# Reordering one stage of a graph-layer kernel: the guess behind the sort, GpSimd's gathers and second secant at the last chunk, a new prologue

## Chip, cores, metric

One core of a Trainium2 chip. The metric is device time in microseconds (us), the median of several executions. Runs of one batch share a chip and the runs of the kernel before that are timed on it. The times differ from chip to chip: the kernel before takes 3235 and 3237 us on two of those used and 3456 us on a third (whether that was the chip or a passing state of it was not tested), so numbers of two batches are compared as ratios or by the loop's own tile length, which is the same (40.95 us in a profile that spans 3454.9 us, 40.93 in one of 3226.0).

## The reference, cut to what matters

Four graph layers on 4096 rows of 256 features, each with a residual and a layernorm. The change lies in the second of two steps of layer 1:

```python
for n in range(2):
    A  = top_p_attention(Xa)   # softmax of q k^T; keep the largest entries of
                               # each row until 90% of its mass; renormalise
    Xf = R @ Xf                # R: sparse adjacency + identity, rows normalised
    Xa = A @ Xa
    Z  = Z + Xf @ U1[n].T + Xa @ U2[n].T
out = layernorm(X + Z)         # then the layer's own residual and layernorm
```

The cut at 90% of the mass is what costs. The kernel finds it per row without sorting 4096 entries: it guesses a bound h from two sums, refines it twice by a secant (each needs two sums over the tile of exponentials), takes 48 candidates below the bound in order, and finds the cut among them.

## The kernel before

Step two works tile by tile (128 rows, 32 tiles) and spreads four tiles over one pass of the loop. While TensorE forms the weighted sum of tile I in eight chunks, the logits of tile I+3 are made, the bound of tile I+2 is refined twice, tile I+1 is sorted and cut, and tile I-1 goes through its projection pz and two layernorms (`end`, in six steps). In this loop the engines run in the order in which the code is written, as the trace has it: VectorE's L754, L881 and L758 start at 2472.09, 2477.39 and 2478.16, and GpSimd's rows below stand in it too.

```python
steps(first); steps(few); run(first)   # tile I+2: secant 1; tile I+1: half the candidates
# slots, one per chunk g of the weighted sum of tile I (TensorE):
#   g 0-3: logits chunk of tile I+3      every g: one matmul of R's sum
#   g 4  : sums for the refinement (L619); end 1     g 5: end 6 of tile I-2
#   g 6  : second of these sums (L621);    end 2 (pz on TensorE)
steps(few)                             # other half of the candidates
if new: guess(new)                     # needs the sums of ALL four logits chunks
new_xa(...); run(r)
if new: run(new["sums"])               # ScalarE: two sums for the guessed bound
run(few)                               # the sort part (VectorE, 8 us)
steps(end)                             # end 3: statistics of pz (VectorE), rs (GpSimd)
ahead = r_ahead(b + 1, got); steps(ahead)   # GpSimd: five gathers for the next R
steps(second)                          # GpSimd: secant 2 of tile I+2, 13 small instructions
c = cut(tile I+1); steps(c)            # VectorE: L754, eight times (e > tie) * e
steps(end)                             # end 4: y = (pz - m) * rs (VectorE L881), GpSimd: * g + x
run(c)                                 # VectorE: match-replace on the whole tile (L758)
steps(end); run(second)                # end 5: statistics of y; new bound h
```

TensorE's next tile begins with the transposes of the tile that was just cut.

## Time and profile before

| | kernel before |
|---|---|
| time | 3234.09 us (3 runs, 3232.30 to 3242.01) |
| step two, one steady tile | 40.95 us |
| VectorE's waits in it | 5.6 us |
| TensorE's wait in it | 10.3 us |

The prediction shows the page's slices, the chain of one tile and VectorE's waits. In all views PE is TensorE, DVE is VectorE, ACT is ScalarE, POOL is GpSimd, and L12 is line 12 of the kernel; rs is one over the standard deviation of a layernorm, st its statistics. One more view belongs beside them: GpSimd's timeline of the same tile (columns are start, length, engine, line, operation, output and inputs; in brackets the idle time before and what ended it).

```profile
2467.68 0.19 POOL L715 COPY f_x<-ex 128x1 f32<-128x1 f32 x1 [4.90 <-DVE ex L714]
...
2470.20 0.57 POOL L240 TENSOR_TENSOR rs<-ve,neg_half 128x1 f32<-128x1 f32 x1
2470.94 1.14 POOL L355 DMA_INDIRECT xg<-xd,idx_x  x1 [0.17 <-issue]
...
2482.63 0.73 POOL L882 TENSOR_TENSOR y<-y,gb 128x256 f32<-128x256 f32 x1
```

The order to see is: a small copy (L715), then rs of the first layernorm (L240), then the gathers (L355), and only behind the second secant the product for y (L882). Here rs stands ahead of everything slow.

### The profile page before, as it was taken

Reading aid. Unit: us, or ns where it says so; the run is one execution under the profiler, and the core shown is the slowest. Engines: PE = TensorE matmul, PEld = TensorE weight load, DVE = VectorE, ACT = ScalarE, POOL = GpSimd, SP = SyncE. Lnnn points to the kernel's source line nnn. Section 1 sums busy time; section 2 is a strip of 40 time slices with the busy share of each in tenths; the row PEclk is TensorE's granted clock in tenths of the full one; section 3 lists DMA queues with packets and bytes.
Section 4 is the critical chain, followed back from the end, with each engine's and each line's share of the span. In section 5 each row is a group of like instructions: output and inputs, shape, how many; then the busy total and the mean of one; then the engine's idle time right before and its main releaser. Section 6 shows DMA issues by size and latency. Waiting matters only on the chain.

```text
span 3454.9 us, 41436 instructions
## 1 busy us (share of the span) xinstructions
PE 2716.3 (79%) x12372; PEld 2045.6 (59%) x12372; DVE 2318.5 (67%) x7296; ACT 1468.8 (43%) x2399; POOL 1539.0 (45%) x2323
## 2 busy tenths in 40 slices
PE   6776778979999999984777777777777766766777
PEld 5554555756767777762565555555555555554665
DVE  5773559956666666615888888888888884554444
ACT  0000013423333433346777776777777751442110
POOL 1025340046555433343655555555555553554553
PEclk9997888989999999996888888888888878788888
DMA  9964440023322222231211111111111103554443
GB/s 293 295 184 142 131 126 30 12 84 105 106 90 92 85 76 66 64 121 44 66 46 54 47 39 36 38 43 38 38 39 34 37 26 116 177 175 147 142 153 102
DMA packets 346506, 322.83 MB, mean 93 GB/s; under 512 B 32032, under 2 KB 305840, under 8 KB 346272
## 3 DMA queue, kind: packets, MB, share of 16 engines
q1 hardware_dynamic: 281696, 187.30, 18.1%
q0 software_dynamic: 43328, 118.63, 11.4%
q10 hardware_dynamic: 21248, 14.16, 1.3%
q8 instruction: 101, 1.65, 0.2%
q14 instruction: 133, 1.09, 0.1%
HBM read 272.48 MB, written 47.48 MB: 93 GB/s over the span
## 4 chain that ended last, share of the span: by engine, by line
PE 22%; DVE 20%; issue 5%; ACT 2%; POOL 2%; another core or an unknown queue 2%; DMA 1%; POOLq 0%; ACTq 0%; DVEq 0%
PE acc L206 6%; DVE e L754 5%; PE lg L515 4%; DVE e L758 4%; PE pt L195 3%; PE acc L925 2%; PE acc L410 2%; DVE top L708 2%; DVE rest L710 2%; PE pz L830 2%; POOL xg L355 1%; PE acc L1124 1%; PE acc L182 1%; ACT e L583 1%
## 5 line engine op out<-in xcount | busy, mean ns | idle before, releaser
L195 PE MATMUL pt<-ident,e 128*128 128x128 f32 x2048 | 328.6, 293 | 347.3 <-DVE e L758 335.1
L355 POOL DMA_INDIRECT xg<-xd,idx_x x360 | 442.3, 1229 | 260.0 <-PE acc L410 107.6
L197 ACT COPY eT<-pt 128x512 f32<-128x512 f32 x512 | 297.0, 588 | 590.0 <-PE pt L195 529.4
L195 PEld LDWEIGHTS pt<-ident,e 128*128 128x128 f32 x2048 | 271.6, 152 | 401.8 <-issue 359.2
L206 PE MATMUL acc<-x,eT 128*128 128x256 f32 x2048 | 499.2, 388 | 0.3 <-ACT eT L197 0.3
L206 PE MATMUL acc<-xa,eT 128*128 128x256 f32 x2048 | 496.0, 389 | 0.0
L206 PEld LDWEIGHTS acc<-x,eT 128*128 128x128 f32 x2048 | 390.3, 194 | 82.2 <-issue 20.7
L206 PEld LDWEIGHTS acc<-xa,eT 128*128 128x128 f32 x2048 | 403.6, 198 | 59.7
L515 PE MATMUL lg<-kT,qi 64*128 64x512 f32 x1024 | 335.0, 718 | 33.5 <-ACT junk L586 23.2
L583 ACT ACTIVATE e<-lg 128x1024 f32<-128x1024 f32 x256 | 262.3, 1025 | 174.4 <-PE lg L515 158.7
L182 PE MATMUL acc<-xw,panel 128*128 128x257 f32 x1024 | 269.4, 414 | 57.7 <-DMA panel<-in_pair 38.8
L410 PE MATMUL acc<-xg,pc 128*128 128x256 f32 x796 | 259.8, 431 | 29.5 <-DMA xg<-x3d,idx_x 11.3
L182 PEld LDWEIGHTS acc<-xw,panel 128*128 128x128 f32 x1024 | 200.7, 205 | 110.7 <-DMA panel<-in_pair 41.0
L687 DVE MAX8 cand<-e 128x8 f32<-128x128 f32 x1024 | 214.9, 279 | 54.2 <-ACT e L583 49.3
L715 POOL COPY f_x<-ex 128x1 f32<-128x1 f32 x64 | 11.8, 184 | 517.9 <-DVE ex L714 517.9
L619 ACT ACTIVATE junk<-e,hm 128x4096 bf16<-128x4096 f32 x64 | 237.2, 3706 | 10.9 <-DVE hm L614 10.2
L621 ACT ACTIVATE junk<-e,h 128x4096 bf16<-128x4096 f32 x64 | 237.7, 3713 | 1.0
L410 PEld LDWEIGHTS acc<-xg,pc 128*128 128x128 f32 x796 | 144.5, 208 | 118.9 <-issue 70.7
L355 POOL DMA_INDIRECT pc<-in_pair,idx_a x180 | 171.6, 953 | 87.0 <-issue 47.5
L696 DVE MAX8 cand<-tmp 128x8 f32<-128x128 f32 x1024 | 204.3, 277 | 2.2
L355 POOL DMA_INDIRECT xg<-x3d,idx_x x146 | 139.1, 953 | 138.9 <-PE acc L410 61.2
L218 ACT COPY xT<-ptx 128x256 f32<-128x256 f32 (+1 forms) x160 | 73.1, 457 | 291.2 <-DMA panel<-in_pair 120.8
(248 smaller groups left out, 4815.1 us busy)
## 6 DMA issues: line engine op xcount, KB each, us to landing
panel<-in_pair SPq DMA_DIRECT2D x200, 256.0 KB
half<-in_pair SPq DMA_DIRECT2D x64, 512.0 KB
pc<-pk SPq DMA_DIRECT2D x55, 320.0 KB
z<-z SPq DMA_DIRECT2D x128, 128.0 KB
pc<-pk SPq DMA_DIRECT2D x45, 256.0 KB
xin<-xd SPq DMA_DIRECT2D x64, 128.0 KB
xg<-xd,idx_x POOLq DMA_INDIRECT x360
pc<-pk SPq DMA_DIRECT2D x23, 192.0 KB
```

Source lines behind the costliest of these rows:

```text
L182: nc.tensor.matmul(ps[:, :width], a[:, k, :], r, start=(j == 0), stop=(j == NT - 1))
L195: nc.tensor.transpose(pt[:, k, :], e[:, (g * 4 + k) * P:][:, :P], ident)
L197: nc.scalar.copy(eT[g], pt)
L206: nc.tensor.matmul(ps[:, :D], eT[g][:, k, :], rhs[j][:, :D], start=(j == 0), stop=(j == NT - 1))
L355: nc.gpsimd.indirect_dma_start(out=o, out_offset=None, in_=src, in_offset=bass.IndirectOffsetOnAxis(ap=idx[:, c], axis=0))
L410: nc.tensor.matmul(ps[:, :width], pc[:, k, :], xs[k][:, :width], start=(n == 0), stop=stop and n == CAPS[I] - 1)
L515: nc.tensor.matmul(ps[:, h, :], qi[r, :], kT[r, (n * NC + c) * LC:][:, :LC], start=True, stop=True)
L583: nc.scalar.activation(both(e, c), ps, AF.Exp, accum_out=s8[:, c:c + 1])
L619: nc.scalar.activation(junk_tile(), e, AF.Relu, bias=hm, accum_out=part)
L621: nc.scalar.activation(junk_tile(), e, AF.Sign, bias=h, scale=-1.0, accum_out=below)
L687: nc.vector.max(cand[:, g, :], e[:, g * SEG:(g + 1) * SEG])
L696: nc.vector.max(cand[:, c * (NS // 2) + g, :], w[:, g * SEG:(g + 1) * SEG])
```

## The change

Its intent: VectorE should not wait 3.7 us per tile for the guess's inputs while it could sort; GpSimd should use its idle time in the middle of the tile; and the prologue should let the first tiles start earlier.

```diff
# loop of step two
+            ahead = r_ahead(b + 1, got) if 0 <= b + 1 < NT else none    # moved up
             if I + 2 < NT: ...
# in the slots
                     steps(r, n_r)
+                    if g == NT // 4 - 1:          # the last chunk
+                        run(r)
+                        steps(ahead)              # gathers
+                        steps(second)             # second secant
# behind the slots
             steps(few)
-            if new:
-                guess(new)
             if I < NT: new_xa(...)
-            run(r)
-            if new:
-                run(new["sums"])
             run(few)                              # sort part
+            if new:
+                guess(new)
+                run(new["sums"])
             steps(end)
-            ahead = ...; steps(ahead)
-            steps(second)
             c = cut(...)
# prologue: for tiles 0, 1, 2 in a loop  ->  tile by tile
-    for I in range(3): start I, guess I, first secant of I-1, ...
-    run(keep_few(at[0])); run(cut(at[0])); run(secant(at[1], 1))
+    start 0, guess 0; start 1, first secant of 0, guess 1, second secant of 0; keep_few 0;
+    start 2, first secant of 1; cut 0; guess 2; second secant of 1
```

## The prediction

> **What bounds the kernel now.** The page first. The change touches only step two, slices 19 to 33, where VectorE reads 8 tenths and TensorE 7, and the prologue just ahead of it.

> ```profile
> PE   6776778979999999984777777777777766766777
> ...
> DVE  5773559956666666615888888888888884554444
> ...
> L195 PE MATMUL pt<-ident,e 128*128 128x128 f32 x2048 | 328.6, 293 | 347.3 <-DVE e L758 335.1
> ```

> The reader sees that no engine is full, and that TensorE's transposes lose 335 us to VectorE's match-replace (L758). So step two is a loop that goes through several engines, and busy shares will not decide it.

> Next the chain that ended last, for one steady tile (times are us of the profiled span; columns are start, length, what).

> ```profile
> 2478.16 4.50 DVE e L758 x2
> ...
> 2482.80 1.94 PE pt L195 x8
> ...
> 2499.45 1.12 ACT e L583 x2
> 2500.57 1.01 ACT junk L586 x2
> ...
> 2501.60 0.17 DVE q L598
> ```

> The loop closes as: match-replace ends the cut of tile I+1, TensorE transposes it, four logits chunks follow among the weighted sum, ScalarE takes the exponentials of the last, VectorE makes the guess from their sums, then sorts and cuts, and the next match-replace ends 40.95 us later (its rows of L754 start at 2472.09 and 2513.05). Third, the waits of VectorE over the steady loop (total us, times, longest).

> ```profile
> DVE f_s L595 <- ACT e L583: 77.4, 27, 3.5
> DVE st L224 <- POOL y L883: 38.9, 27, 2.0
> DVE q L598 <- ACT junk L586: 22.9, 27, 0.8
> ...
> DVE st L224 <- PE pz L876: 0.8, 3, 0.3
> ```

> The first and third rows are what the change aims at: (77.4 + 22.9) / 27 = 3.7 us per tile, as the guess stands ahead of the sort on VectorE and holds it up. The second, 1.4 us, is the wait for GpSimd's layernorm product. The last row is my main warning: VectorE already waits now and then for the projection pz of the previous tile, so that result comes only just in time.

> To see how just, I took TensorE's, ScalarE's and GpSimd's timelines of the same tile (one row each; columns are start, length, engine, line). I count all times below from the end of match-replace at 2482.66.

> ```profile
> 2509.39 0.59 PE L876 MATMUL pz<-z,ident 128*128 128x256 f32 x2
> ```
> ```profile
> 2508.40 3.71 ACT L621 ACTIVATE junk<-e,h 128x4096 bf16<-128x4096 f32 x1
> ```
> ```profile
> 2477.71 0.19 POOL L629 TENSOR_SCALAR below<-below 128x1 f32<-128x1 f32 x1
> ```

> pz is complete at 2509.98 = 27.3. The second refinement's sums (L621, with a 0.19 us accumulator read) end at 2512.20 = 29.5. The second secant on GpSimd is 13 small instructions, from 2477.71 to 2482.67: 4.96 us with nothing in the way. VectorE reaches the eight cutting instructions (L754) at 2513.05 = 30.4 and leaves them 5.39 later, at 35.8.

> [...] within the hand-scheduled loop all four engines run exactly in the order in which the program emits. [...] in the first tile's cut:

> ```profile
> 1612.51 5.38 DVE L754 SCALAR_TENSOR_TENSOR e<-e,ties 128x512 f32<-128x512 f32 x8
> ```
> ```profile
> 1615.95 2.00 POOL L629 TENSOR_SCALAR below<-below 128x1 f32<-128x1 f32 x1 [6.59 <-ACT junk L621]
> ```

> That GpSimd instruction normally takes 0.19 us (the 2477.71 row). Here it started under L754 and ended at 1617.95, just as the eighth ended (1617.89). At 1657.34 in the next cut, one slipped in at a border between two of the eight (0.49 us) and its successor was held again (1.32 against 0.34). Match-replace has one input, and the secant runs at its usual pace beside it.

> **The change, part by part.**

> 1. Guess behind the sort. VectorE's second half of the candidates ends at 2497.7 = 15.0. The sort no longer waits: it takes 2502.25 to 2510.20 = 8.0, so it ends at 23.0; the guess is five instructions of 0.2, done at 23.9 (its inputs were there at 18.9). Removed: 3.7 us of waiting. But the next thing in VectorE's order is the statistics of pz, which come at 27.3. TensorE's order has not changed and it runs without a gap from 0.1, so VectorE waits 3.4 us there, and L754 starts at 30.3 instead of 30.4. Gain on the path: about 0.1 us. ScalarE gains nothing: the guess's sums still follow the second refinement's sums and the copy-out of the weighted sum (31.3).

> 2. GpSimd. The five gathers move from 28 to 35 into a gap in which GpSimd idles (6.0 us at 2494.85 to 2500.85): good. The 13 secant instructions now also stand before the guess's six, the f_x copy and the rs pair of the first layernorm. Before, rs was ready at 2511.73 = 29.1, well ahead of the row "y L881" that needs it, which stands between L754 and match-replace. Now:
> - the secant can start when L621 ends, 29.5; two instructions get through by 30.3;
> - L754 then holds the rest until 35.8, but for perhaps three that slip in at borders (from the two cuts quoted);
> - left are 8 to 11 instructions, 2.9 to 4.3 us: 38.7 to 40.1;
> - f_x 0.3, the guess's six 2.2 (1648.20 to 1650.43), ve and rs 0.9 (2510.84 to 2511.73): 42.1 to 43.5;
> - VectorE's y 0.5, drop 0.25, match-replace 4.5: the cut ends at 47.3 to 48.7.
> So the loop takes 6.4 to 7.7 us longer per tile; I take 7.0. Tiles 1 to 29 have both a second secant and a layernorm of the tile before: 29 x 7.0 = +203 us. The 1.4 us behind match-replace goes away (y's two products of 0.73 each, rows L882 and L883, fit beside match-replace), yet it lies off the path, in VectorE's slack.

> 3. Prologue. Before, tile 0's first secant was computed at 1553.6 but its h was written at 1567.46, behind the guess of tile 1; the first cut ended at 1622.4, and in the first loop tile VectorE waited 7.6 us for tile 1's second secant. Tile by tile, ScalarE's sums of tile 0 ended at 1549.0, the exponentials of tile 1 are 8.8 (4 x 2.2), its own second sums 7.7: about 1575; second secant 5, candidates and sort 18.5, cut 12.3: about 1611. That is -11, and the 7.6 us goes mostly too, as the other sums then fit on ScalarE ahead of it: -18 in all. This part is reordered by the scheduler, so -5 to -30.

> Sum, in profiled time: 203 - 18 = +185 us. The profiled run takes 3455 against 3234 unprofiled; I scale by that ratio, 0.936, to +173, and predict 3405 us.

> **The rivals.**
> - The intended gain: both VectorE waits vanish and the tile falls to VectorE's busy time, 40.95 - 5.65 of idle = 35.3. That would be 29 x 5.6 = -162 us, with the prologue some 3066. It needs pz five us earlier, and nothing in the change gives it that.
> - A wait that merely takes the old one's place: pz holds the sort's end, GpSimd is in time. Then only the prologue counts, about 3215. For it: the pz row above. Against it: it needs rs within 35.8, while the 8.3 us of GpSimd work behind L621 make 37.8 even with nothing blocked.
> - GpSimd late, but not blocked by L754: rs at 37.8, cut ends 43.1, +2.1 per tile, +61 - 18 = +43: about 3275, "within 2%". Against it is the 2.00 us row.

> **Range and chances.** With three or more slips at borders and a good prologue (5.5 per tile, -30) I get about 3355; with none (7.7, -5) about 3440. The unblocked rival and doubt whether profiled waits carry over widen it downward: 3290 to 3450. Slower by over 2% 0.82, within 2% 0.12 (both milder rivals), faster 0.06.

> **What would show it.** Right: the f_s and q waits (L595, L598) gone; "st L224 <- PE pz" grown to some 3 us per tile; a new VectorE wait at y L881 for rs of 5 to 8 us; GpSimd's secant rows inside L754 at 0.5 to 2 us each or one of some 5; the tile period 47 to 49; TensorE's wait for match-replace 7 us longer. The prologue's first match-replace ends 10 to 25 us sooner after the last step-one row. Wrong: if the loop's emission order were not kept on GpSimd, or L621 ended some 8 us sooner, rs would be in time and the second rival's 3215 would come.

## The result, and the profile after

| | before | after |
|---|---|---|
| time, median | 3234.77 us (4 runs) | 3329.86 us (4 runs, 3325.14 to 3333.29) |
| ratio | | 1.0289 (1.0268 to 1.0310) |
| steady tile | 40.95 us | 44.35 us |

Ratios here and below are the mean time of one kernel's fast runs over that of the other's of the same rounds, so not quite the ratio of the medians. The changed kernel is slower by 95 us; the prediction said 3405, some 170 us slower.

Where the 95 us are can be read from the match-replace rows (count, min/median/max ns, first and last start). First a fresh profile of the kernel before, which spans 3226 us, then the changed kernel:

```profile
L758 DVE MATCH_REPLACE8 e<-drop,e x32: 4402/4408/4411, 1519.6 to 2778.4; 128x4096 f32<-128x4096 f32 x32
```
```profile
L758 DVE MATCH_REPLACE8 e<-drop,e x32: 4403/4408/4411, 1518.1 to 2880.3; 128x4096 f32<-128x4096 f32 x32
```

From the first to the last: 1258.8 and 1362.2 us, so the loop costs +103. From the last keep instruction of step one (1377.8 and 1385.5) to the first match-replace: 141.8 and 132.6, so the prologue gives -9. Sum +94.

VectorE's waits over the steady loop of the changed kernel:

```profile
DVE y L881 <- POOL rs L240: 104.7, 22, 4.8
DVE st L224 <- PE pz L876: 92.4, 22, 4.7
```

The waits for the guess's inputs are gone, and beside the two rows shown 8.1 us are left in all. The two stand in their place: 4.2 us per tile for pz (92.4 over 22) and 4.8 us for rs (104.7 over 22). TensorE's row of the page grew with them (the last number is the wait that match-replace ended):

```profile
L195 PE MATMUL pt<-ident,e 128*128 128x128 f32 x2048 | 328.2, 293 | 459.7 <-DVE e L758 439.7
```

Its wait for match-replace rose from 335.1 to 439.7 us, over 31 tiles 3.4 us each. VectorE's timeline of one tile has both new waits in brackets:

```profile
2084.07 0.43 DVE L224 BATCH_NORM_STATS2 st<-pz 128x6 f32<-128x256 f32 x1 [4.17 <-PE pz L876]
...
2086.86 5.42 DVE L754 SCALAR_TENSOR_TENSOR e<-e,ties 128x512 f32<-128x512 f32 x8
2097.03 0.54 DVE L881 TENSOR_SCALAR y<-pz,mv,rs 128x256 f32<-128x256 f32 x1 [4.75 <-POOL rs L240]
```

The chain of one tile, which went from the logits to the guess before, now goes through ScalarE's second sums and GpSimd:

```profile
2102.45 1.94 PE pt L195 x8
...
2126.90 3.71 ACT junk L621 x2
...
2140.80 0.58 POOL rs L240
```

GpSimd's timeline of a tile tells why rs is late:

```profile
2086.34 0.18 POOL L629 TENSOR_SCALAR below<-below 128x1 f32<-128x1 f32 x1 [11.05 <-ACT junk L621]
...
2087.07 0.71 POOL L629 TENSOR_SCALAR na<-f,tgt 128x1 f32<-128x1 f32 x1
...
2088.50 1.21 POOL L629 TENSOR_SCALAR dm<-f,b 128x1 f32<-128x1 f32 x1
...
2093.67 0.18 POOL L715 COPY f_x<-ex 128x1 f32<-128x1 f32 x1
2093.92 0.23 POOL L597 TENSOR_SCALAR tgt<-f_s 128x1 f32<-128x1 f32 x1
...
2096.43 0.57 POOL L240 TENSOR_TENSOR rs<-ve,neg_half 128x1 f32<-128x1 f32 x1
```

The second secant waits 11.05 us for ScalarE's sums. It then runs under the eight L754 instructions (2086.86 to 2092.28) at 0.53 to 1.21 us for six instructions that take 0.26 to 0.58 beside match-replace in the kernel before. Only then come the copy (L715), the guess's six (from L597) and, last, rs, which ends at 2097.00; y starts at 2097.03.

### The profile page after: what moved, and what is told of

It reads as the page before. It is cut to its first block, busy times and chain, and to the rows that moved or that the text cites. A ratio compares the mean times of both kernels' runs of the same rounds, so it can differ in the third digit from the quotient of the medians.

```text
span 3323.3 us, 41439 instructions
## 1 busy us (share of the span) xinstructions
PE 2629.2 (79%) x12372; PEld 1990.4 (60%) x12372; DVE 2305.1 (69%) x7296; ACT 1468.3 (44%) x2399; POOL 1593.7 (48%) x2323
## 3 DMA queue, kind: packets, MB, share of 16 engines
q1 hardware_dynamic: 281696, 187.30, 18.9%
## 4 chain that ended last, share of the span: by engine, by line
PE 56%; DVE 11%; POOL 11%; ACT 8%; DMA 8%; issue 5%; ACTq 0%; POOLq 0%; DVEq 0%; SPq 0%
PE acc L206 20%; PE lg L515 8%; PE pt L195 7%; PE acc L410 5%; DVE e L758 4%; DMA half<-in_pair 4%; PE acc L182 4%; ACT junk L621 3%; PE pz L830 3%; ACT junk L619 3%; PE acc L925 2%; PE acc L1125 2%; POOL dm L629 2%; POOL pc L355 1%; POOL xg L355 1%
## 5 line engine op out<-in xcount | busy, mean ns | idle before, releaser
L195 PE MATMUL pt<-ident,e 128*128 128x128 f32 x2048 | 328.2, 293 | 459.7 <-DVE e L758 439.7
L195 PEld LDWEIGHTS pt<-ident,e 128*128 128x128 f32 x2048 | 271.4, 152 | 514.5 <-issue 471.1
L355 POOL DMA_INDIRECT xg<-xd,idx_x x360 | 426.6, 1185 | 271.0 <-PE acc L410 97.4
L206 PE MATMUL acc<-xa,eT 128*128 128x256 f32 x2048 | 483.2, 381 | 5.0 <-ACT eT L197 4.8
L206 PEld LDWEIGHTS acc<-xa,eT 128*128 128x128 f32 x2048 | 389.8, 192 | 58.5 <-ACT eT L197 5.8
L583 ACT ACTIVATE e<-lg 128x1024 f32<-128x1024 f32 x256 | 262.0, 1023 | 160.9 <-PE lg L515 160.7
L621 ACT ACTIVATE junk<-e,h 128x4096 bf16<-128x4096 f32 x64 | 237.6, 3712 | 1.0
L715 POOL COPY f_x<-ex 128x1 f32<-128x1 f32 x64 | 11.6, 181 | 369.4 <-DVE ex L714 369.4
L754 DVE SCALAR_TENSOR_TENSOR e<-e,ties 128x512 f32<-128x512 f32 x256 | 173.4, 745 | 1.2
```

The source lines that it names most:

```text
L195: nc.tensor.transpose(pt[:, k, :], e[:, (g * 4 + k) * P:][:, :P], ident)
L206: nc.tensor.matmul(ps[:, :D], eT[g][:, k, :], rhs[j][:, :D], start=(j == 0), stop=(j == NT - 1))
L355: nc.gpsimd.indirect_dma_start(out=o, out_offset=None, in_=src, in_offset=bass.IndirectOffsetOnAxis(ap=idx[:, c], axis=0))
L583: nc.scalar.activation(both(e, c), ps, AF.Exp, accum_out=s8[:, c:c + 1])
L621: nc.scalar.activation(junk_tile(), e, AF.Sign, bias=h, scale=-1.0, accum_out=below)
```

## The experiments

Twelve runs, in three batches of four: 1 to 4, then 5 to 7 with 12, then 8 to 11. Theory Q is the prediction's: the second secant, put ahead of rs on GpSimd, which keeps the order of the code, makes rs late.

### 1. The second secant back

The changed kernel, with:

```diff
                         steps(ahead)
-                        steps(second)
...
             steps(end)
+            steps(second)
             c = cut(...)
```

> The changed kernel with one thing undone: the second secant goes back on GpSimd behind the guess's instructions and the first layernorm's rs; the early gathers, the guess behind the sort and the new prologue stay. Theory Q (the second secant, waiting for ScalarE's sums at the head of GpSimd's in-order queue, makes rs late): the wait of VectorE's y for rs disappears, the tile falls from 44.4 to 39.8 to 41.0 us, what is left bounds it at the wait for pz, and the time is 3205 to 3235 us. Rival G (rs is late because the late guess's six instructions now stand ahead of it): most of the wait for rs stays, time above 3290. Rival I (the intended gain was there and only hidden): below 3150.

Measured: 3212.23 us, ratio to before 0.9924 (0.9899 to 0.9949). Of VectorE's waits one above 9 us in all is left:

```profile
DVE st L224 <- PE pz L876: 127.5, 25, 6.0
```

No wait for rs is left; pz is what it waits for, 5.1 us per tile. This one line carries the whole loss. Theory Q stands; the intended gain of some 100 us did not appear. The time is some 11 us below what runs 3 and 4 add up to. The early gathers may have brought it, or the parts do not simply add up (see "The beat"); no run tells these apart.

### 2. The guess ahead again

The changed kernel, with the guess and its sums back ahead of the sort:

```diff
             steps(few)
+            if new: guess(new)
             ...new_xa...
+            if new: run(new["sums"])
             run(few)
-            if new: guess(new); run(new["sums"])
```

> The changed kernel with only the guess and its sums put back ahead of the sort; the second secant and the gathers stay at the last chunk. Theory Q: rs is as late as in the changed kernel, since the guess's GpSimd instructions still stand behind the second secant and ahead of rs: 3315 to 3345 us. Rival G (the late guess did it): the wait for rs goes, 3215 to 3240 us.

Measured: 3331.55 us, ratio 1.0302, the same as the changed kernel.

```profile
DVE y L881 <- POOL rs L240: 104.7, 22, 4.8
DVE f_s L595 <- ACT e L583: 74.0, 23, 3.4
```

The wait for rs is to the tenth what it was, and the old wait for the guess's inputs is back beside it at no cost. So the late guess is not to blame (rival G), and in the changed loop its wait is not on the path either.

### 3. The late guess alone

The kernel before with only the guess moved behind the sort.

```diff
             steps(few)
-            if new: guess(new)
             ...
-            if new: run(new["sums"])
             run(few)
+            if new: guess(new); run(new["sums"])
```

> The kernel before with only the guess and its sums moved behind the sort. Theory P (pz is the next thing VectorE waits for): the wait for the guess's sums of 3.7 us per tile turns into a wait for pz of about 3.5 us, and the time is within 10 us of before, 3222 to 3240 us. Rival I (what the change intended): 29 tiles times 3.7 us less, 3110 to 3140 us.

Measured: 3229.43 us, ratio 0.9982 (0.9974 to 0.9989): 6 us, of the 107 that the wait would have been worth.

```profile
DVE st L224 <- PE pz L876: 93.2, 24, 4.5
```

The 3.7 us of waiting for the guess turned into 3.9 us (93.2 over 24) for pz.

### 4. The new prologue alone

The kernel before with the changed kernel's prologue lines and nothing else.

> The kernel before with only the new prologue. From the two traces the stretch between the last keep instruction of step one and the first match-replace shrank from 147.2 to 132.7 us; so 3212 to 3228 us, 0.2 to 0.7 per cent faster. If the loop's slots fall differently and take it back, 3230 to 3240.

Measured: 3228.82 us, ratio 0.9983 (0.9976 to 0.9990), just short of the expected range. The stretch up to the first match-replace did shrink (132.9 us; 141.8 in the fresh profile of before), but the loop's first tile grew from 40.8 to 45.2 us: about half was given back at once. In the first two tiles VectorE waits for a guess's inputs twice, 13.0 us together, where before it waited once, 7.2 us; I did not follow that further.

### 5. The cut with one input

Does the cut really hold up GpSimd? The changed kernel, with L754 reading e once; its result is wrong on purpose.

```diff
-scalar_tensor_tensor(eg, eg, ties[:, g:g+1], eg, op0=is_gt, op1=mult)
+tensor_scalar(eg, eg, ties[:, g:g+1], 0.0, op0=is_gt, op1=add, accum_out=cnt[:, g:g+1])
```

> The changed kernel with the eight cutting instructions (L754) written with one SBUF input instead of two; the result is wrong on purpose (kept entries become ones), order, sizes and waits stay. Theory L (the cut [...] stretches the second secant from 4.96 to 7.4 us): the secant runs at 4.9 to 5.1 us beside the cut, VectorE's wait for rs falls from 4.8 to 2.2 to 2.6 us, and the time is 3250 to 3275 us if the new instructions last as long. Rival: the secant is slow for another reason (busy VectorE or ScalarE in general): still 7.4 us, 3320 to 3340 us.

Measured: 3284.70 us, ratio 1.0135 (1.0107 to 1.0164). The new instructions are recorded with 0.74 us each, the old ones with 0.75. GpSimd's second secant beside them, its first and its last row:

```profile
2116.50 0.18 POOL L629 TENSOR_SCALAR below<-below 128x1 f32<-128x1 f32 x1 [11.05 <-ACT junk L621]
...
2121.12 0.30 POOL L629 TENSOR_SCALAR b<-b,far 128x1 f32<-128x1 f32 x1
```

It takes 4.92 us (2116.50 to 2121.42) instead of 7.4, and the wait for rs fell to 2.3 us. So the cut does hold up GpSimd: order, sizes and length stayed, and what changed is the number of inputs, two with 7.4 us and one with 4.92 (the new form also writes a small sum). But the time fell by some 50 us (the ratio from 1.0289 to 1.0135), not by the 55 to 80 expected, and the tiles came out uneven: 43.1, 42.1, 43.2, 42.1 us in turn. That was the first sign of something that I had left out.

### 6. The statistics of pz behind match-replace

If pz is what holds the loop once the secant is back, nothing in the way of the cut should wait for pz or rs. From run 1:

```diff
-            steps(end)             # end 3: statistics of pz, rs
             steps(second)
-            c = cut(...); steps(c)
-            steps(end)             # end 4: y
-            run(c)
-            steps(end)             # end 5
+            c = cut(...); run(c)   # cut and match-replace together
+            steps(end)             # end 3, behind match-replace
             run(second)
# ends 4, 5, 6 of that tile move into the next pass: behind the first half of the
# candidates, behind the second half, behind the sort
```

> The kernel with the second secant back, and in addition the first layernorm's statistics of pz behind match-replace and its later steps in the next tile, so that nothing in the cut's way waits for pz or rs. Theory P (pz is what holds the loop there, 5.1 us of waiting per tile of 40.2): the tile falls to 35.5 to 37 us, near VectorE's busy 35, and the time to 3080 to 3130 us. Rival (the next bound lies close: ScalarE's sums and the first secant, or GpSimd): tile 38 to 40, time 3150 to 3210 us.

Measured: 3077.03 us, ratio 0.9500 (0.9473 to 0.9526), correct. This beats both kernels. The engines' busy time over some 25 tiles (us, instructions; engines in the order of the first line):

```profile
core 0: us, PE busy (x) PEld busy (x) DVE busy (x) ACT busy (x) POOL busy (x), PEclk, DMA share, GB/s
1706.60:2600.00 893.40, 754.68 (x3477) 568.09 (x3476) 851.30 (x2629) 722.67 (x868) 579.92 (x1144) 0.91 0.15 45
```

VectorE is busy 851 of 893 us, 95%. The tile is 34.8 us, and it and the time lie a little under the lower end of what was expected; VectorE's own work now all but sets them.

### 7. The same with the guess ahead

> As the run with the statistics behind match-replace, but the guess and its sums ahead of the sort again. Theory (two chains of nearly one length close the loop, one through pz and one through the guess; either alone still holds it): last exponentials 18.9, guess 0.9, sort 8.0, cut 12.4 make a tile of 40.2 us, so 3200 to 3225 us. Rival (pz alone was the bound): 3080 to 3130 us as without the guess ahead.

The edit is run 6 with guess and sums ahead of the sort. Measured: 3232.96 us, ratio 0.9982 (0.9974 to 0.9990): the late guess, worth 6 us by itself in run 3, is worth 156 us here. Two chains close the loop, and each alone holds it.

```profile
DVE f_s L595 <- ACT e L583: 111.3, 22, 5.1
DVE q L598 <- ACT junk L586: 18.6, 22, 0.8
```

The wait for the guess's inputs is 5.9 us per tile ((111.3 + 18.6) over 22). But the expectation was 3200 to 3225, from a tile of 40.2 us, and the tile is 40.95 to 40.98 us, tile after tile: the very length of the kernel before, by another chain.

### The beat

Why should such different loops have the same tile? The tile lengths, from successive match-replace starts of late tiles (us):

```
before            40.95 40.96 40.96 40.96 40.97 40.95 40.96 40.96
run 7             40.97 40.95 40.96 40.95 40.97 40.98 40.97
run 2             44.37 44.35 44.37 44.36 44.37 44.39 44.38 44.38
run 1             39.25 40.06 40.50 40.73 | ... | 39.29 40.06 40.51 40.73 40.85
```

```profile
2482.80 1.94 PE L195 MATMUL pt<-ident,e 128*128 128x128 f32 x8 [10.31 <-DVE e L758]
2484.67 2.08 PE L515 MATMUL lg<-kT,qi 64*128 64x512 f32 x4
...
2487.69 2.51 PE L206 MATMUL acc<-xa,eT 128*128 128x256 f32 x8
```
```profile
2102.45 1.94 PE L195 MATMUL pt<-ident,e 128*128 128x128 f32 x8 [14.96 <-DVE e L758]
2104.32 1.93 PE L515 MATMUL lg<-kT,qi 64*128 64x512 f32 x4
```

Eight transposes take 1.94 us where four take 0.60 later; four logits matmuls 1.9 to 2.1 instead of 1.1; so TensorE starts every tile of these two at half speed. Before, the slow part reaches into the first eight of the weighted sum: 2.31 us on the chain where eight take 1.73, about 2.7 of them slow, so it ends 6.3 us after the start. Changed, it ends within the logits, 3.5 us after the start. If the change to full speed comes at this beat, a tile that starts later by d has a slow part shorter by d and gets half of d back. Then a tile is drawn towards a multiple of the beat, and its distance from it halves from tile to tile. Run 1 shows just this: 40.96 less 39.25, 40.06, 40.50, 40.73 is 1.71, 0.90, 0.46, 0.23. I call this theory K; the last four runs test it.

The granted clock bears theory K out. The half-speed part of a steady tile ends 6.2 us after TensorE's start before and 3.5 after, close to what the durations gave. The clock also shows what ends the halving in run 1: the slow parts of successive tiles last 3.0, 4.7, 5.6, 6.1 and 6.3 us, and then the part is one beat shorter again. Two tiles in turn, from TensorE's start to the change (columns as in run 6; the third number from the end is the granted clock):

```profile
1932.20:1938.48 6.28, 6.28 (x18) 4.00 (x19) 6.13 (x22) 3.29 (x6) 5.00 (x10) 0.50 0.00 0
1973.03:1976.02 2.99, 2.99 (x12) 2.05 (x12) 2.89 (x6) 1.17 (x2) 2.41 (x2) 0.50 0.00 0
```

### 8 and 9. The same delay in both kernels

```diff
         yield                                   # in cut(), ahead of match-replace
+        for _ in range(2): nc.vector.max(idle8, rest)   # 0.89 us, never read
```

> The kernel before with two idle MAX8 of 0.44 us each (together 0.89 us, nothing reads them) on VectorE ahead of match-replace, so squarely on the path that ends the tile. Theory K (TensorE, idle for 10 us per tile, starts at half speed and changes to full speed at a fixed beat of 3.413 us, so the tile locks to 40.96 us = 12 beats and a later start is paid back by a shorter slow stretch): the tile stays at 40.96, the slow stretch shrinks by 1.8 us, and the time stays within 5 us of before, 3230 to 3242 us. Rival S (plain sum of durations): tile 41.85, 31 tiles, 3255 to 3270 us.

Measured on the slower chip: 3464.34 us against 3456.36, ratio 1.0026 (1.0012 to 1.0040): +9 us. The late tiles are 40.95, 40.95, 40.96, 40.98 us: the delay costs nothing there. The clock shows why: the slow part is 4.5 us instead of 6.2, shorter by about twice the delay. Most of what it costs is in the first tiles, which have not yet reached the beat: 41.92, 43.23, 41.69, 41.33 us, 4.8 us over those of the fresh profile before. A plain sum would have made +26 to +28 us. The time is 4 us above the band that theory K gave (within 5 us of before); its tile length is as stated.

> The changed kernel with the same 0.89 us at the same place. Theory K: there the tile is 44.37 us = 13 beats with a slow stretch of only 3.6 us, [...], so nothing more can be paid back; the tile leaves the 44.37 and lies between 45.1 and 46.8 us, uneven from tile to tile; time 3350 to 3395 us. Rival S: tile 45.25, even, 3352 to 3362 us; if 44.37 were held as in the kernel before, 3325 to 3335.

Measured: 3598.17 us, ratio to before 1.0413 (1.0378 to 1.0449), where the changed kernel alone had 1.0289 on another chip: 0.0124 x 3456 = about +43 us. Tiles: 45.38, 45.33, 46.09, 45.29, 46.48, 45.42 us, uneven, some 45.7 in the mean; some tiles, of 44.9, lie a little under the expected 45.1. By the clock their slow parts jump between 3.0 and 6.4 us. The same 0.89 us costs nothing in one kernel and 1.3 us per tile in the other, more than itself. A plain sum can give neither.

### 10 and 11. TensorE kept busy

```diff
             run(slot)
+            # 20 (before) or 30 (changed) matmuls of 128x256, results never read
+            for _ in range(20): nc.tensor.matmul(wt[:, :D], ident, Xa1[0][:, :D], start=True, stop=True)
```

> The kernel before with 20 idle matmuls (128x256, results never read) behind each weighted sum, which fill 8.6 us of TensorE's wait for the next cut. Theory K: TensorE stays at full speed, its first instructions of a tile take 0.9 instead of 1.9 us and so on, pz comes 3.1 us sooner, and the tile falls to 37.5 to 38.5 us; time 3140 to 3175 us. Rival (the slow start is hidden, or is not due to idling): tile 40.9, time 3230 to 3240, or more if the idle matmuls get in the way.

Measured: 3378.47 us, ratio 0.9775 (0.9737 to 0.9813). The tile is 38.02 us, even, on no multiple of the beat. TensorE's rows, from the idle matmuls (L1060; each of the 20 leaves two records) on:

```profile
2106.94 8.80 PE L1060 MATMUL warm<-xa,ident 128*128 128x256 f32 x40
2117.40 1.06 PE L195 MATMUL pt<-ident,e 128*128 128x128 f32 x8 [1.67 <-DVE e L758]
2118.39 1.13 PE L515 MATMUL lg<-kT,qi 64*128 64x512 f32 x4
```

The eight transposes take 1.06 instead of 1.94 us. Work that nobody needs makes the kernel faster by 78 us, and each tile by 2.9 of 40.96 us, 7%, as the slow start lies on the path (faster is clear; whether by more than 2% is not, since the interval ends at 0.9813). Theory K holds, in time and in tile.

> The changed kernel with 30 such idle matmuls (13 us), as its TensorE waits 14 us. Theory K: the slow stretch of 3.6 us goes, the tile falls by half of it, 1.8 us, to 42.2 to 42.9 us, time 3265 to 3285; against the kernel before with idle matmuls the change then costs 4.3 to 5.0 us per tile, more than the 3.4 us that the locked tiles show. Rival: 44.4 us, 3325 to 3335.

Measured: 3534.97 us, ratio to before 1.0240 (1.0202 to 1.0279), against 1.0289 without: about -17 us, a third of what was expected. The trace shows both answers. Six of tiles 2 to 9 take 42.71 to 42.73 us and the other two 43.1 to 43.2; from tile 10 on nearly all are 44.3 to 44.4 again. In those, a slow stretch is back, but it is another one: the eight transposes still take 1.06 us, and the four logits matmuls after them take 1.93. So where the filling holds, the change costs 42.7 - 38.0 = 4.7 us per tile, as theory K said; that it stops holding I had not foreseen.

The length of TensorE's wait alone does not explain it. It is 2.05 us in the slow tiles, and 2.04 to 2.07 in four of the eight that stay fast. What differs is where the wait lies in the beat. In tile 10 it falls within one beat for the first time; the next beat runs at half clock (columns as in run 6):

```profile
2040.48:2043.89 3.41, 1.35 (x11) 1.04 (x12) 3.31 (x6) 0.52 (x2) 0.60 (x2) 1.00 0.14 42
2043.89:2047.31 3.42, 3.42 (x8) 1.65 (x7) 3.39 (x10) 2.17 (x5) 3.12 (x4) 0.50 0.00 0
```

TensorE is busy 1.35 of 3.41 us there, 40%; in the tile before, the wait was split over two beats, and the emptier one was busy 54%. The traces of the kernel before and of the changed kernel agree: from 1640 to 2700 us, TensorE was busy for 33% or less in each of the 50 full-speed beats that were followed by one at half speed, and for 49% or more in each of the 375 that were followed by another at full speed. Once the loop has taken 44.37 us, 13 beats, every later wait falls at the same place in its beat, and so the slow beat returns in every tile.

### 12. The kernel before once more

> The kernel before once more, for a second profile: its first profile spans 3455 us against 3234 unprofiled, and the changed kernel's 3323 against 3330. If the first profile was an odd run in the stages that the change does not touch, this one spans 3225 to 3245 with a tile of 40.9 us in the loop; if profiling always slows this kernel, 3440 to 3470.

Measured: 3227.77 us, one run, whose state is not known; its profile spans 3226.0 us, with tiles of 40.93 us in the mean. So it is the first case: profiling does not slow this kernel. The first profile, 3454.9 us, fits the slower chip of runs 8 to 11, where the kernel before takes 3456 us unprofiled.

## Why the prediction was right, and where its sizes were off

The direction, the range and the mechanism held; the size was 1.8 times too large. That the range held was in part luck: the least that the prediction's own mechanism gave was "about 3355", and 3330 lies below it. It lies in the range only since this was widened downward for other reasons, a rival and a doubt about profiled waits.

1. "The guess behind the sort": right. The wait went and one for pz came, 4.2 us (predicted 3.4); alone it is worth 6 us (run 3), and undone it costs nothing (run 2).
2. "GpSimd": right in kind. The y L881 wait for rs came as named, 4.8 us (predicted 5 to 8), and run 1 shows that it is the whole loss. The tile was said to end at 47.3 to 48.7 and ended at 44.35. Counted from the end of match-replace:

| term | predicted | measured |
|---|---|---|
| L621 ends | 29.5 | 28.3 |
| second secant, from there | 9.2 to 10.6 | 7.4 |
| copy, guess, rs | 3.4 | 3.3 |
| y, drop, match-replace | 5.25 | 5.3 |
| tile | 47.3 to 48.7 | 44.35 |

The two terms that were mis-sized: first, "L754 then holds the rest until 35.8, but for perhaps three that slip in". Six ran under it, so the two-input cut cost 2.5 us (7.4 against run 5's 4.92) and not the 4.2 to 5.6 that the prediction assumed. Second, L621: the prediction took TensorE's stretch of the tile over unchanged, and it became 1.2 us shorter, since a tile that starts at another point of the beat has a shorter slow part (3.5 instead of 6.3 us; half the difference is 1.4). Runs 8 and 10 show that this part depends on the clock: pz, complete 27.3 us after match-replace before and 26.1 in the changed kernel, comes at 26.5 with the delay of run 8 and at 24.4 with run 10's filling. The prediction had no such step.

3. Prologue, "-18 in all": the stretch gave 9 us, and run 4 shows that 6 remain once the first loop tile has paid. The term that failed is the 7.6 us at the first tile: in run 4 that wait is still 4.9 us, and the waits for a guess's inputs beside it grew by 5.8. A sum of this part is wrong too, as it is written: 1549.0 + 8.8 + 7.7 is 1565.5 and not "about 1575"; carried through, the stretch would have shrunk by some 21 us, further from the 9 measured.
4. The scaling by 0.936 was baseless. Run 12 shows that profiling costs nothing here; the first profile came, it seems, from a slower chip, and the loop is equally long on both, so there was nothing to scale. It moved the forecast by 12 us, by luck towards the measured time.

Of the rivals, the second ("a wait that merely takes the old one's place", some 3215) is what run 1 measured, 3212, once GpSimd was put in order. The first, the intended gain, needed "pz five us earlier"; run 6 got it by no longer waiting for pz ahead of the cut. What remains open: why the second tile of the changed kernel takes 51.9 us (42.6 before), and what the early gathers bring alone.

## What to carry to other kernels

When you move work earlier on an engine that keeps the order of the code, as GpSimd does here, ask what it waits for and who stands behind it: here a secant that waited 11 us was put ahead of a 0.6 us result that VectorE needed. When a wait goes and the time stays, look for the second chain of the same length; a change that is worth nothing alone (run 3) can be worth 5% together with the one that frees the other chain (runs 6 and 7). And where TensorE idles in every pass of a loop, look at its granted clock, and whether the pass is a multiple of the beat on which it changes, as 40.96 and 44.37 us were of 3.413 here: a small loss then need not show in the time (0.89 us per tile in run 8 left the tile at 40.95 to 40.98), and runs that differ by it may not be told apart.
